# A two-layer Perceiver block on one core: turned context rows kept in memory for cross attention, image rows in parts of 512, 512 and 500

## The chip, the cores and the metric

The kernel runs on one core of one Trainium2 chip. The metric is device time in microseconds (us) of one execution. TensorE multiplies matrices, VectorE (DVE) does reductions and elementwise work, ScalarE (ACT) evaluates functions and copies, GpSimd (POOL) issues the indirect gathers, and SyncE (SP) issues most loads. SP and ACT each feed one DMA queue (q1 and q10 in the profile), POOL feeds q0; all of them run on the same 16 DMA engines.

## What is computed

There are 16 batches of 64 latent rows of width 256 and one context of 1601 rows of width 256 per batch: 77 text rows first, then 1524 image rows. All values are float32.

```python
x = x + deformable_cross_attention(layernorm(x), ctx)   # layer 0: K, V of all 1601 context rows, 5 sampled rows per head and query
x = x + sigmoid_self_attention(layernorm(x))
x = x + moe_gelu(layernorm(x))                          # 8 experts, 2 chosen
x = x + cross_attention(layernorm(x), ctx)              # layer 1, 16 heads of 64:
#   softmax over the 77 text rows + softmax over the 1524 image rows, each with its own K and V weights
x = x + state_space_block(layernorm(x))
x = x + moe_swiglu(layernorm(x))                        # 32 experts, 4 chosen, and a shared one
```

The change touches two places that read the same context: the projection of all context rows to keys and values in layer 0, and the image half of the cross attention in layer 1.

## The kernel before

The latents are 8 tiles of 128 rows (two batches each) that stay in on-chip memory (`x4`). The order of the instructions on TensorE, DVE and ACT is written out by hand; SP and POOL are ordered by a planner, which takes instructions in the order of the program as their buffers become free in its own reckoning, so SP can run ahead of the compute engines until a load's buffer isn't free. Each engine then runs its list strictly in order, the issuing of DMAs included.

**Key/value stage** (`keys_values`, lines 386 to 428). The context is cut into `spans` (line 237): per batch three spans of 512 rows and one of the 65 rows left over. A span of 512 is loaded to the tile `cx` with 4 neighbouring rows in each of 128 partitions (`cx_load`, three buffers, on SP). A span is worked on in steps of two row groups: TensorE transposes blocks of 128 x 128 (`transposes`, line 153), ACT copies them to `cxt` (line 415, three buffers), and one span later `project` multiplies them by the joint weights of all heads (`st<-wkv,cxt`, line 88, into one of four PSUM banks `st`) and ACT copies keys and values to `kv` (line 399, four buffers). When a span is complete, ACT issues its write to a table in memory (`tab`, line 402, one table for two batches), 512 bytes for each head and group of four rows. There are 7 such steps in a batch. Beside them run, in the same hand-written order: the sampling positions, the gathers of table rows (POOL, line 446, released by DVE's copy `ig`, line 444), the attention on gathered rows (`attend`), the text keys and values for layer 1 (`texts`), and, later, the dense part of layer 0 for the first tiles (`attention`, `middle`, whose weights are the tiles `w`). `tick` paces gathers and attention: it counts planned microseconds, starts a gather every 16 of them and places the attention 42 after its second gather.

**Change of stage** (lines 1590 to 1613). The pool `kvp` is given back, pools `xq` and `xc` take its memory, `cr.loads(0)` loads the image rows of batch 0, the remaining `mids` run, and `cr.begin` prepares the first pair of heads.

**Cross attention** (`class Cross`, lines 924 to 1202). A step `n` handles batch `n // 8` and a pair of heads, 128 steps in all. The image rows lie on chip twice. `cn` (two buffers, loaded by `loads` one batch ahead) has them as rows, 11 neighbouring rows per partition plus a last group of 116 partitions with one row, and a column of ones. `cT` (one buffer) has them transposed, made from `cn` by `turn`: 24 transposes on TensorE into PSUM, evicted by DVE and ACT. A step computes 12 blocks of scores from `cT` and the folded queries `qf` (three `st` banks of 4 blocks), takes maxima on DVE (line 1107), turns them (line 1126) and broadcasts them (line 1136), subtracts (line 1147), exponentiates on ACT (line 1148), and multiplies the exponentials `pt` of the step before with `cn` (`product`, line 1076). In the last step of a batch (`hp == 7`), after `out`, `turn` makes the next batch's `cT` (line 1119); `begin` makes the first one. Some steps carry parts of the next tiles' layers (`side`, `mid`, `more`, `late`).

Of the kernel before, what the change touches and what calls it, by code (L numbers as in the profile page):

```python
# [11 lines left out]
AF = mybir.ActivationFunctionType  # L12
ALU = mybir.AluOpType
# [4 lines left out]
P = 128  # L18
B, S, D = 16, 64, 256
M = 1601  # L20
# [14 lines left out]
H1, HD1, INNER, TEXT = 16, 64, 1024, 77  # L35
IMG = M - TEXT
NHP = H1 // 2
CM = IMG // P
CR = IMG - CM * P
NCH = CM + 1  # L40
NB = NCH // 4


NST, NCONV = 16, 4
# [21 lines left out]
def perceiver_kernel(ctx: ExitStack, tc: tile.TileContext, a: dict, out: bass.AP):  # L66
    nc = tc.nc

    def mk(pool, shape, tag, dtype=F32, bufs=None):
        return pool.tile(list(shape), dtype, tag=tag, name=tag, bufs=bufs)  # L70
# [9 lines left out]
    def copy(i, o, x):  # L80
        if i % 2:
            nc.scalar.copy(o, x)  # L82
        else:
            nc.vector.tensor_copy(o, x)

    def mm(o, pairs):
        for i, (l, r) in enumerate(pairs):
            nc.tensor.matmul(o, lhsT=l, rhs=r, start=i == 0, stop=i == len(pairs) - 1)  # L88
# [59 lines left out]
    def transposes(blocks, ncol=P):  # L148

        rows = blocks[0].shape[0]  # L150
        t = bank().rearrange("p (i n) -> p i n", n=P)
        for i, b in enumerate(blocks):
            nc.tensor.transpose(t[:ncol, i, :rows], b, ident[:rows, :rows])  # L153
        return t
# [79 lines left out]
    sp = tpp  # L234


    spans = [(b, m0, RP if M - m0 >= RP * P else 1) for b in range(B) for m0 in range(0, M, RP * P)]
    cxs = {}

    def cx_load(i):  # L240
        if i < len(spans):
            b, m0, r = spans[i]
            w = min(P, M - m0)
# [142 lines left out]
    def keys_values():  # L386

        held = kv = None

        def project(i, cxt, q):  # L390
            nonlocal kv
            b, m0, r = spans[i]
            w = min(P, M - m0)
            if q == 0:
                kv = mk(kvp, [P, H0, RP, 2 * HD0], "kv", bufs=4)
            for c in range(2 * q, min(2 * q + 2, r)):
                pk = big()
                mm(pk[:w], [(cxt[:, c, k, :w], wkv[:, k, :]) for k in range(KC)])
                nc.scalar.copy(kv[:w, :, c, :], pk[:w].rearrange("p (h e) -> p h e", h=H0))  # L399
            if 2 * q + 2 >= r:  # L400
                tab = tables[b // 2].rearrange("n e -> (n e)").rearrange("(b h m e) -> b h m e", b=2, h=H0, e=2 * HD0)
                nc.scalar.dma_start(
                    out=tab[b % 2, :, m0 : m0 + w * r, :].rearrange("h (p r) e -> p h (r e)", r=r),
                    in_=kv[:w, :, :r, :].rearrange("p h r e -> p h (r e)"),
                )

        for i, (b, m0, r) in enumerate(spans):
            w = min(P, M - m0)
            cx = cxs.pop(i)
            cxt = mk(kvp, [P, RP, KC, P], "cxt", bufs=3)  # L410
            steps = (r + 1) // 2
            for q in range(steps):
                m = min(2, r - 2 * q)
                tp = transposes([cx[:w, 2 * q + t, k * P : (k + 1) * P] for t in range(m) for k in range(KC)])
                nc.scalar.copy(  # L415
                    cxt[:, 2 * q : 2 * q + m, :, :w].rearrange("p r k n -> p (r k) n"), tp[:, : KC * m, :w]
                )
                if q + 1 == steps:
                    cx_load(i + 3)
                if held:  # L420
                    for part in range((held[2] + 1) // 2):
                        if min(part, steps - 1) == q:
                            project(held[0], held[1], part)
                yield
            held = (i, cxt, r)
        for q in range((held[2] + 1) // 2):
            project(held[0], held[1], q)
        yield
# [495 lines left out]
    class Cross:  # L924
# [7 lines left out]
        def loads(self, b):  # L932
            if b >= B:
                return

            cn = self.cn[b] = mk(self.xc, [P, NCH, D + 1], "cn", bufs=2)
            nc.gpsimd.memset(cn[:, :, D:], 1.0)  # L937
            nc.sync.dma_start(
                out=cn[:, :CM, :D], in_=a["ctx"][b, TEXT : TEXT + CM * P, :].rearrange("(p c) d -> p c d", c=CM)
            )  # L940
            nc.sync.dma_start(out=cn[:CR, CM, :D], in_=a["ctx"][b, TEXT + CM * P :, :])

        def text_loads(self, b):
            if b >= B:
# [9 lines left out]
        def turn(self, b):  # L954

            if b >= B:
                return
            cn = self.cn[b]
            ct = self.ctx[b] = mk(self.xc, [P, KC, NCH * P], "cT", bufs=1)
            i = 0  # L960
            for k in range(KC):
                d = slice(k * P, (k + 1) * P)
                for c in range(0, CM, 4):
                    n = min(4, CM - c)
                    blocks = [cn[:, c + i_, d] for i_ in range(n)]
                    tp = transposes(blocks)
                    copy(i % 3, ct[:, k, c * P : (c + n) * P].rearrange("p (i n) -> p i n", n=P), tp[:, :n, :])
                    i += 1
                tp = transposes([cn[:CR, CM, d]])
                nc.scalar.copy(ct[:, k, CM * P : IMG], tp[:, 0, :CR])  # L970

                nc.scalar.copy(ct[:, k, IMG:], ct[:, k, : NCH * P - IMG])

        def queries(self, t, part):

# [94 lines left out]
        def product(self, n, part, po):  # L1070

            b = n // NHP
            pt, cn = pts[n % 2], self.cn[b]
            for c in range(part * 4, part * 4 + 4):
                w = P if c < CM else CR
                nc.tensor.matmul(po, lhsT=pt[:w, c, :], rhs=cn[:w, c, :], start=c == 0, stop=c == NCH - 1)  # L1076

        def turn_out(self, n):
# [8 lines left out]
        def step(self, side=None, mid=None, more=None, late=None):  # L1087
# [11 lines left out]
            for i in range(NB):  # L1099
                if live:  # L1100
                    s = big().rearrange("p (c n) -> p c n", n=P)
                    for c in range(4):
                        j = (i * 4 + c) * P
                        mm(s[:, c, :], [(ct[:, k, j : j + P], qf[:, k, :]) for k in range(KC)])
                    st.append(s)
                if live:
                    nc.vector.tensor_reduce(mp_[:, i, :], s.rearrange("p c n -> p n c"), AX.X, ALU.max)  # L1107
                    if i:
                        nc.vector.tensor_tensor(mp_[:, 0, :], mp_[:, 0, :], mp_[:, i, :], ALU.max)
                if i == 1 and n - 2 < last:  # L1110
# [30 lines left out]
            if live:  # L1141
                pt = pts[n % 2]
                for i in range(NB):
                    c0 = i * 4
                    m = 4 if i + 1 < NB else 3
                    o = pt[:, c0 : c0 + m, :]
                    nc.vector.tensor_tensor(o, st[i][:, :m, :], mc.to_broadcast([P, m, P]), ALU.subtract)  # L1147
                    nc.scalar.activation(o, o, AF.Exp)  # L1148
                o = pt[:CR, CM, :]
                nc.vector.tensor_tensor(o, st[-1][:CR, 3, :], mc[:CR, 0, :], ALU.subtract)  # L1150
                nc.scalar.activation(o, o, AF.Exp)
            if late is not None:
                next(late, None)
            if old:
# [29 lines left out]
        def begin(self, xp):  # L1184
            self.xp = xp
            self.text_loads(0)
            self.weights(0, 0)
            yield
            for part in range(3):
                self.queries(0, part)  # L1190
                yield
            self.turn(0)
            self.loads(1)
            yield
            self.text(0, 0)
# [348 lines left out]
    with tc.manual_schedule(engines={ET.PE, ET.DVE, ET.Activation}):  # L1544
# [49 lines left out]
        for i in range(2):  # L1594
            qbds.append(mk(xq, [P, NHP, 2, 2, S], f"qbd{i}"))
            nc.gpsimd.memset(qbds[i], 0.0)
            pts.append(mk(xq, [P, NCH, P], f"pt{i}"))
            nc.gpsimd.memset(pts[i][:, CM, :], 0.0)
        xc = sx.enter_context(tc.tile_pool(name="xc", bufs=1))
        cr = Cross(xc)  # L1600
        cr.loads(0)
        while mids:
            if attended() < mids[0][0]:
                tick(2.4)
            mid()
# [156 lines left out]
```

## Time and profile before

| what | us |
|---|---|
| median of 3 runs | 3048.33 (3040.24 to 3052.96) |
| profiled execution, its own time | 3041.33 |
| its span, first to last instruction | 3039.6 |
| TensorE busy | 2840.8 |
| key/value stage | 0 to 589.5 |
| rest of the first tiles' layer 0 | 589.5 to 763 |
| cross attention steps | 763 to 2743 |

The span is the time from the first to the last instruction of the one execution that the profiler recorded. "Busy" is the union of an engine's instructions; matmuls are pipelined, so the duration of one (278 ns for a score matmul) is longer than its share of the time. Every float32 matmul shows as two instructions; a transpose is one. A square bracket in a timeline row gives the engine's idle time before the instruction and what ended it. In the DMA view a queue's row gives its packets, the megabytes, and the time of its packets as a share of what 16 engines have. The packets of four bytes among them are the completion writes of a transfer.

### The profile page before, as it was taken

The numbers are of one execution on the slowest core, as the hardware profiler recorded it, in microseconds if no ns is written. First come the engines' busy times: TensorE is split into PE (matmuls) and PEld (weight loads), VectorE is DVE, ScalarE is ACT, GpSimd is POOL, SyncE is SP. The second block draws the span as 40 slices with busy tenths as digits, with TensorE's granted clock in tenths as the row PEclk, the third lists the DMA queues.
The fourth block names the chain that finished last, engine by engine and source line by source line (L and its number), as shares of the span: only waits on it lengthen the run. The fifth ranks groups of instructions, "written<-read, shape, count | busy, mean of one in ns | idle before, by whom it ended". The sixth has DMA issues, their size and how long they took to land.

```text
span 3039.6 us, 46506 instructions
## 1 busy us (share of the span) xinstructions
PE 2840.8 (93%) x17734; PEld 2354.4 (77%) x17734; DVE 1615.9 (53%) x4137; ACT 1032.8 (34%) x2375; POOL 816.6 (27%) x923
## 2 busy tenths in 40 slices
PE   8999999966999998789979999999999999998889
PEld 4554446656898987679979999899999999886666
DVE  3332133244676665533236765686544785646756
ACT  3433444333223223324323332343233442222421
POOL 0655545566677720000010110011000010002620
PEclk9999999978999999899989999999999999999999
DMA  7666856636121220135512111122111221004983
GB/s 227 175 195 215 245 166 178 200 111 185 31 69 50 71 82 18 40 105 178 186 53 75 45 55 60 28 81 68 37 33 46 61 67 50 8 1 153 293 240 112
DMA packets 337608, 326.05 MB, mean 107 GB/s; under 512 B 58966, under 2 KB 288634, under 8 KB 336874
## 3 DMA queue, kind: packets, MB, share of 16 engines
q1 hardware_dynamic: 184889, 225.11, 23.5%
q10 hardware_dynamic: 126928, 63.06, 7.2%
q0 software_dynamic: 25568, 34.91, 5.2%
q8 instruction: 141, 2.31, 0.3%
q14 instruction: 82, 0.66, 0.1%
HBM read 248.37 MB, written 74.62 MB: 106 GB/s over the span
## 4 chain that ended last, share of the span: by engine, by line
PE 80%; DVE 9%; DMA 4%; ACT 3%; issue 1%; POOL 1%; ACTq 0%; SPq 0%; DVEq 0%; POOLq 0%
PE st L88 34%; PE mm L1076 21%; PE mm L88 16%; PE mm L153 5%; PE mm L1032 2%; DMA wg<-in_guT 2%; POOL g L446 1%; PE mm L1062 1%; DVE mp L1107 1%; DVE hs L1315 1%; PE mm L1001 1%; PE mm L1126 1%; DMA yk<-y0d,sli 1%; DVE pt L1147 1%; ACT pt L1148 0%
## 5 line engine op out<-in xcount | busy, mean ns | idle before, releaser
L1076 PE MATMUL mm<-cn,pt 128*128 128x257 f32 (+1 forms) x3072 | 748.8, 388 | 0.2 <-ACT cT L82 0.2
L88 PE MATMUL st<-qf,cT 128*128 128x128 f32 x6144 | 741.2, 278 | 0.9 <-ACT qf L1035 0.9
L446 POOL DMA_INDIRECT g<-tab,ig x640 | 613.8, 959 | 467.5 <-DVE ig L444 181.5
L88 PEld LDWEIGHTS st<-qf,cT 128*128 128x128 f32 x6144 | 722.8, 195 | 5.4 <-ACT qf L1035 1.5
L1076 PEld LDWEIGHTS mm<-cn,pt 128*128 128x128 f32 (+1 forms) x3072 | 559.5, 192 | 84.5 <-issue 0.8
L88 PE MATMUL st<-wkv,cxt 128*128 128x512 f32 (+1 forms) x832 | 380.1, 602 | 3.3 <-ACT cxt L415 3.3
L1107 DVE TENSOR_REDUCE mp<-st 128x128 f32<-128x512 f32 x384 | 260.4, 687 | 213.3 <-PE st L88 212.9
L1147 DVE TENSOR_TENSOR pt<-st,mc 128x512 f32<-128x512 f32 (+1 forms) x384 | 224.0, 638 | 159.0 <-ACT mc L1138 159.0
L88 PEld LDWEIGHTS st<-wkv,cxt 128*128 128x128 f32 (+1 forms) x832 | 150.8, 190 | 162.6 <-issue 158.4
L1148 ACT ACTIVATE pt<-pt 128x512 f32<-128x512 f32 (+1 forms) x384 | 208.0, 588 | 52.1 <-DVE pt L1147 51.8
L399 ACT COPY kv<-st 128x512 f32<-128x512 f32 (+1 forms) x208 | 121.7, 587 | 202.2 <-PE st L88 201.1
L1138 ACT COPY mc<-mm 128x128 f32<-128x128 f32 x128 | 34.2, 267 | 398.8 <-PE mm L1136 398.3
L1085 ACT COPY ot<-mm 128x256 f32<-128x256 f32 x128 | 47.6, 372 | 343.3 <-PE mm L153 343.2
L937 POOL MEMSET cn<- 128x12 f32 x16 | 1.9, 122 | 527.1 <-PE mm L1076 517.3
L1128 DVE TENSOR_REDUCE xmx<-mm 128x1 f32<-128x128 f32 x128 | 37.3, 291 | 185.5 <-PE mm L1126 185.5
L1405 POOL DMA_INDIRECT xb<-xnd,row x55 | 55.7, 1013 | 263.0 <-PE mm L1062 223.3
L1321 POOL TENSOR_TENSOR mn<-mn,hc 128x512 f32<-128x512 f32 x64 | 81.6, 1274 | 160.7 <-DVE hc L1320 156.6
L1052 ACT COPY yt<-mm 128x64 f32<-128x64 f32 x128 | 27.2, 213 | 252.6 <-PE mm L88 252.6
L88 PE MATMUL mm<-xt,w 128*128 128x256 f32 (+1 forms) x512 | 94.1, 336 | 6.8 <-DMA w<-in_gate 4.6
L88 PEld LDWEIGHTS mm<-xt,w 128*128 128x128 f32 x512 | 82.5, 200 | 22.6 <-issue 10.0
L153 PEld LDWEIGHTS mm<-ident,cx 128*128 128x128 f32 (+1 forms) x416 | 52.9, 145 | 42.1 <-issue 28.4
L1315 DVE TENSOR_TENSOR_SCAN hs<-da,db 128x512 f32<-128x512 f32 x64 | 78.4, 1225 | 6.6
(455 smaller groups left out, 3885.9 us busy)
## 6 DMA issues: line engine op xcount, KB each, us to landing
tab<-kv ACTq DMA_DIRECT2D x48, 1024.0 KB
w<-in_gate SPq DMA_DIRECT2D x66, 512.0 KB
cx<-in_ctx SPq DMA_DIRECT2D x48, 512.0 KB
cn<-in_ctx SPq DMA_DIRECT2D x16, 1408.0 KB
wg<-in_guT SPq DMA_DIRECT2D x87, 256.0 KB
w<-in_lin SPq DMA_DIRECT2D x33, 512.0 KB
wk<-in_xwkiT SPq DMA_DIRECT2D x32, 512.0 KB
wd<-in_down1T SPq DMA_DIRECT2D x87, 128.0 KB
```

What stands on the lines that cost most here:

```text
L88: nc.tensor.matmul(o, lhsT=l, rhs=r, start=i == 0, stop=i == len(pairs) - 1)
L153: nc.tensor.transpose(t[:ncol, i, :rows], b, ident[:rows, :rows])
L399: nc.scalar.copy(kv[:w, :, c, :], pk[:w].rearrange("p (h e) -> p h e", h=H0))
L446: nc.gpsimd.indirect_dma_start(out=gf[:, (half * n + s) * 4 * HD0 : (half * n + s + 1) * 4 * HD0], out_offset=None, in_=tables[j], in_offs ...
L1032: nc.tensor.matmul(pf[:, k * P : (k + 1) * P], lhsT=w[:, hp % 4, k * P : (k + 1) * P], rhs=rhs, start=True, stop=True)
L1076: nc.tensor.matmul(po, lhsT=pt[:w, c, :], rhs=cn[:w, c, :], start=c == 0, stop=c == NCH - 1)
L1107: nc.vector.tensor_reduce(mp_[:, i, :], s.rearrange("p c n -> p n c"), AX.X, ALU.max)
L1147: nc.vector.tensor_tensor(o, st[i][:, :m, :], mc.to_broadcast([P, m, P]), ALU.subtract)
L1148: nc.scalar.activation(o, o, AF.Exp)
L1315: nc.vector.tensor_tensor_scan(hs.rearrange("p c n -> p (c n)"), da.rearrange("p c n -> p (c n)"), db.rearrange("p c n -> p (c n)"), 0.0, ...
L1321: nc.gpsimd.tensor_tensor(y, y, hc, ALU.add)
L1405: nc.gpsimd.indirect_dma_start(out=x, out_offset=None, in_=xnd, in_offset=bass.IndirectOffsetOnAxis(ap=tb.row[:, i : i + 1], axis=0))
```

## The change

The text rows become a span of their own, first in each batch (77 rows, one per partition), and the image rows become three spans: 512, 512 and 500 rows, the last with 125 partitions of four rows (`SPAN = (P, P, 125)`). The counts of spans, steps, transposes and projections in a batch stay as they are. After the last step of an image span, ACT also issues a write of the whole `cxt` (512 KB, 128 partitions) to a new tensor `ctd` in memory; in the span of 125 partitions it first fills the three columns left over with copies of the first three.

In cross attention the transposes of `turn` go. `turn` now issues three loads of 512 KB on SP, one for each part, into tiles `ct0` to `ct2` with one buffer each. Batch 0's are issued right after `cr.loads(0)`, no longer in `begin`. `cn` is laid out as the spans are, by three loads with 128, 128 and 125 partitions instead of two with 128 and 116; there are 12 blocks as before. The softmax works on three whole groups of four blocks, where it had two groups of four, one of three and one single block, and the memset of `pt` goes.

```diff
-CM = IMG // P
-CR = IMG - CM * P
-NCH = CM + 1
-NB = NCH // 4
+SPAN = (P, P, 125)
+NB = len(SPAN)
+NCH = NB * RP
...
-    spans = [(b, m0, RP if M - m0 >= RP * P else 1) for b in range(B) for m0 in range(0, M, RP * P)]
+    spans = [(b, m0, w, r) for b in range(B) for m0, w, r in [(0, TEXT, 1)] + [(TEXT + s * RP * P, w, RP) for s, w in enumerate(SPAN)]]
+
+    ctd = mk(dram, [B, NB, P, RP * KC * P], "ctd")
...
                 nc.scalar.copy(
                     cxt[:, 2 * q : 2 * q + m, :, :w].rearrange("p r k n -> p (r k) n"), tp[:, : KC * m, :w]
                 )
+                if r > 1 and w < P:
+
+                    nc.scalar.copy(
+                        cxt[:, 2 * q : 2 * q + m, :, w:].rearrange("p r k n -> p (r k) n"), tp[:, : KC * m, : P - w]
+                    )
                 if q + 1 == steps:
                     cx_load(i + 3)
+                    if r > 1:
+                        nc.scalar.dma_start(out=ctd[b, (m0 - TEXT) // (RP * P)], in_=cxt.rearrange("p r k n -> p (r k n)"))
...
-            nc.sync.dma_start(
-                out=cn[:, :CM, :D], in_=a["ctx"][b, TEXT : TEXT + CM * P, :].rearrange("(p c) d -> p c d", c=CM)
-            )
-            nc.sync.dma_start(out=cn[:CR, CM, :D], in_=a["ctx"][b, TEXT + CM * P :, :])
+            m0 = TEXT
+            for i, w in enumerate(SPAN):
+                nc.sync.dma_start(
+                    out=cn[:w, i * RP : (i + 1) * RP, :D], in_=a["ctx"][b, m0 : m0 + w * RP, :].rearrange("(p r) d -> p r d", r=RP)
+                )
+                m0 += w * RP
...
-            cn = self.cn[b]
-            ct = self.ctx[b] = mk(self.xc, [P, KC, NCH * P], "cT", bufs=1)
-            i = 0
-            for k in range(KC):
-                d = slice(k * P, (k + 1) * P)
-                for c in range(0, CM, 4):
-                    n = min(4, CM - c)
-                    blocks = [cn[:, c + i_, d] for i_ in range(n)]
-                    tp = transposes(blocks)
-                    copy(i % 3, ct[:, k, c * P : (c + n) * P].rearrange("p (i n) -> p i n", n=P), tp[:, :n, :])
-                    i += 1
-                tp = transposes([cn[:CR, CM, d]])
-                nc.scalar.copy(ct[:, k, CM * P : IMG], tp[:, 0, :CR])
-
-                nc.scalar.copy(ct[:, k, IMG:], ct[:, k, : NCH * P - IMG])
+            self.ctx[b] = [
+                load(self.xc, f"ct{i}", ctd[b, i].rearrange("p (r k n) -> p r k n", r=RP, k=KC), [P, RP, KC, P], 1) for i in range(NB)
+            ]
...
-                w = P if c < CM else CR
+                w = SPAN[c // RP]
...
-                        j = (i * 4 + c) * P
-                        mm(s[:, c, :], [(ct[:, k, j : j + P], qf[:, k, :]) for k in range(KC)])
+                        mm(s[:, c, :], [(ct[i][:, c, k, :], qf[:, k, :]) for k in range(KC)])
...
                 for i in range(NB):
-                    c0 = i * 4
-                    m = 4 if i + 1 < NB else 3
-                    o = pt[:, c0 : c0 + m, :]
-                    nc.vector.tensor_tensor(o, st[i][:, :m, :], mc.to_broadcast([P, m, P]), ALU.subtract)
+                    o = pt[:, i * 4 : i * 4 + 4, :]
+                    nc.vector.tensor_tensor(o, st[i], mc.to_broadcast([P, 4, P]), ALU.subtract)
                     nc.scalar.activation(o, o, AF.Exp)
-                o = pt[:CR, CM, :]
-                nc.vector.tensor_tensor(o, st[-1][:CR, 3, :], mc[:CR, 0, :], ALU.subtract)
-                nc.scalar.activation(o, o, AF.Exp)
...
-            self.turn(0)
             self.loads(1)
...
-            nc.gpsimd.memset(pts[i][:, CM, :], 0.0)
         xc = sx.enter_context(tc.tile_pool(name="xc", bufs=1))
         cr = Cross(xc)
         cr.loads(0)
+        cr.turn(0)
```

More of the change, by code (lines that the diff above doesn't have):

```diff
@@ L241, in cx_load @@
         if i < len(spans):
-            b, m0, r = spans[i]
-            w = min(P, M - m0)
+            b, m0, w, r = spans[i]
             cx = cxs[i] = mk(kvp, [P, RP, D], "cx", bufs=3)
@@ L391, in project @@
             nonlocal kv
-            b, m0, r = spans[i]
-            w = min(P, M - m0)
+            b, m0, w, r = spans[i]
             if q == 0:
@@ L405, in project @@
                 )
-        for i, (b, m0, r) in enumerate(spans):
-            w = min(P, M - m0)
+        for i, (b, m0, w, r) in enumerate(spans):
             cx = cxs.pop(i)
```

## The prediction

> **What bounds the kernel now.** The page first: TensorE is busy 93% of the span and holds 80% of the chain that ended last, so time leaves only through TensorE, and a delay counts only where TensorE ends up waiting for it.
>
> ```profile
> PE 2840.8 (93%) x17734; PEld 2354.4 (77%) x17734; DVE 1615.9 (53%) x4137; ACT 1032.8 (34%) x2375; POOL 816.6 (27%) x923
> PE 80%; DVE 9%; DMA 4%; ACT 3%; issue 1%; POOL 1%; ACTq 0%; SPq 0%; DVEq 0%; POOLq 0%
> ```
>
> Then the timeline of TensorE at a batch's end in cross attention. The transposes of `turn` stand bare between two groups of matmuls:
>
> ```profile
> 2619.27 0.45 PE L88 MATMUL mm<-ot,wvi 128*64 128x64 f32 x6
> 2619.65 2.96 PE L153 MATMUL mm<-ident,cn 128*128 128x128 f32 x24
> 2622.53 2.01 PE L1076 MATMUL mm<-cn,pt 128*128 128x257 f32 x8
> ```
>
> They take 2.88 us from start to next start. Read likewise, the fifteen boundaries inside the stage take 2.88 to 3.75 us, 47.5 us in sum.
>
> Third, the key/value stage (0 to 589.5 us) cut at the end of each batch, since the change loads it. Columns: stretch and its length; busy time of PE, PEld, DVE, ACT, POOL; granted clock; mean share of the 16 DMA engines; GB/s.
>
> ```profile
> 42.40:75.50 33.10, 33.10 (x125) 19.36 (x124) 15.14 (x52) 11.31 (x21) 0.00 (x0) 1.00 0.67 193
> 179.10:223.10 44.00, 44.00 (x158) 26.57 (x157) 14.56 (x48) 17.25 (x36) 17.71 (x19) 1.00 0.57 175
> 308.50:338.10 29.60, 26.27 (x77) 12.39 (x76) 6.49 (x21) 11.02 (x21) 13.22 (x14) 0.94 0.90 271
> 338.10:363.20 25.10, 25.10 (x81) 12.21 (x80) 6.29 (x19) 11.20 (x21) 12.60 (x13) 1.00 0.77 214
> 388.40:429.10 40.70, 36.36 (x116) 19.31 (x115) 17.01 (x54) 15.40 (x29) 19.18 (x20) 0.92 0.51 144
> ```
>
> TensorE is full, but the DMA engines are used 51 to 90%: this is where the change can turn the bound. Where they reach 0.90, TensorE already loses 3.3 us, by way of an issue that holds ScalarE's queue for 5.92 us:
>
> ```profile
> 305.86 0.37 ACTq L402 DMA_DIRECT2D tab<-kv  x1
> ...
> 308.54 5.92 ACTq L402 DMA_DIRECT2D tab<-kv  x1
> 314.49 1.07 ACT L415 COPY cxt<-mm 128x512 f32<-128x512 f32 x2 [6.82 <-issue]
> ```
>
> **Removed: `turn`.** Fifteen boundaries give back 47.5 us. The row maxima (two DVE steps, 0.69 and 0.29 us) must then be ready within `out` and the first product (0.65 + 1.74 us); where DVE is behind, steps without a turn show gaps of 0.24 us, so I leave 1 us: **-46.5**. The sixteenth turn, in `begin`, has 1.69 us on the chain: **-1.7**. Its evictions (64 DVE copies, 39.7 us; 96 on ACT, 33.7 us) lie under TensorE: 0. Likewise the softmax in three whole groups: DVE 128 x (684 - 547 - 279) ns = -18 us, ACT -22 us, both hidden by the product of the pair before: 0.
>
> **Added in cross attention.** Per batch three 512 KB reloads on SP's queue. Each part has one buffer, free once the last pair's scores have read it: about 2, 4 and 6 us into a step of 15.6 - 2.9 = 12.8 us, and needed 12.8, 14.7 and 16.6 us after that start. An isolated 512 KB load (`wk`, issued 1013.05) has its last packet 3.5 us after issue. Waiting behind the reloads on SP: the next `wk`, `cn`, `vt`, needed a step or more later. Margin over 6 us: 0, with 5 us per late boundary if SP stands in another wait.
>
> **Added in the key/value stage.** ACT issues 48 writes of 512 KB (0.37 us each) and makes 32 small copies (0.21 us, as L972): 24 us over 590 us in which ACT is busy 42%; hidden by the four `st` buffers, some 6 us of matmuls. The transfers are another matter. DMA views of two short stretches, one holding a 128-row table write (48 such) and a 128-row `cx` load, one a 65-row table write:
>
> ```profile
> q10 hardware_dynamic: 2064, 1.05, 44.7%
> q1 hardware_dynamic: 144, 0.52, 21.7%
> ```
>
> ```profile
> q10 hardware_dynamic: 1053, 0.13, 10.0%
> ```
>
> 2064 is 128 x 16 packets of 512 B and 16 more; 144 is 128 and 16; but 1053 is 65 x 16 = 1040 and **13** more. The extra ones are completion writes, one from each engine that took part: 65 rows were spread over 13 engines, not 16. A third stretch with 128-, 77- and 116-row loads agrees (1632 = 1408 + 16 + 77 + 11 + 116 + 4). The Trainium skill says this as a rule (DMA: Bandwidth & Descriptors, section "Why a DMA increments its semaphore by 16 and not by 1"): a copy uses the largest number of engines up to 16 that divides the size of its slowest dimension. No 125-row transfer is in the trace. Going by the nearest row in size (128 rows, 16 engines), the new spans cost what the old ones do; going by the rule, which three counts support, **125 = 5 x 5 x 5 gets five engines**. I take the rule; the row would lead to rival (a), 3015 us.
>
> From those rows (8 us stretch): a 1 MB table write is 0.447 x 8 = 3.58 us of all 16 engines, a 512 KB load in 4 KB packets 0.217 x 8 = 1.74 us. On five engines the 125-row table write takes 3.58 x 16/5 x 125/128 = 11.2 us, the `cx` load 5.4 us. What a batch adds to each of these five:
> - table write of the third part: 11.2 - 3.6 = 7.6 us
> - its `cx` load: 5.4 - 1.7 = 3.7 us
> - three turned writes (128 partitions, all engines; priced as loads): 3 x 1.74 = 5.2 us
> - text of 77 rows on 11 engines for 65 on 13: 0.5 us
>
> Together 17 us, on top of share x length: 22.2 + 17 = 39.2 us in a 33.1 us stretch, 19.3 + 17 = 36.3 in 25.1, 26.6 + 17 = 43.6 in 29.6, 25.1 + 17 = 42.1 in 44.0. Over the sixteen stretches what exceeds the length adds to 82 us, less 7 because the first batch's third write falls into the second: 75 us if the five engines never idle. They must idle some: **+80** (bounds 40, if packets run faster with eleven engines quiet, and 125). Buffers can't absorb it: three `cxt`, four `kv`, and ACT's queue itself, where an issue waits for room and cxt copies, `kv` copies and the activations of the feed-forward wait behind it, and TensorE for them.
>
> **Moved: text first.** The same seven steps a batch, in another order, with the same transposes, matmuls and copies: 0. POOL's first gather (79.0 us) waits for the last table write of batch 1, now one of 11 us; the attention that uses it is placed 42 us of planned time behind it, so 0, and at most the delay of some 9 us if that cover were gone. `turn(0)` moves up to the end of this stage and onto SP's queue, its source long written. And the last write of the stage is now the slow one. At the change of stage SP waits for it, the loads following in order:
>
> ```profile
> 592.73 0.65 SPq L938 DMA_DIRECT2D cn<-in_ctx  x1
> 593.44 1.15 SPq L941 DMA_DIRECT2D cn<-in_ctx  x1
> 594.69 4.08 SPq L158 DMA_DIRECT2D w<-in_gate  x2
> ...
> 604.04 2.18 PE L88 MATMUL mm<-xt,w 128*128 128x256 f32 x9 [2.22 <-DMA w<-in_gate]
> ```
>
> `cn` waits for the table writes (memory reused), released at 592.65, 3.2 us after the last issue; with 11.2 us of transfer that is some 9 us later. Three turned loads (5.2 us) go ahead of `w`, and `cn`'s 125-row part costs 3 us on five engines. TensorE waits for `w`: 0 to 18 us, **+14**.
>
> **Sum.** -46.5 - 1.7 + 80 + 14 = +45.8. The profiled execution took 3041.3 us (span 3039.6), giving 3087; it stands 7 us under the median of three, so the forecast for a median is 3048.3 + 45.8 = **3094 us**, its own range 3065 to 3130.
>
> **Rivals.** (a) The 125-row transfers spread as 128-row ones, or the surplus hides. Then the stage adds 4.8 us per engine and batch, which fits below 1.0 nearly everywhere (some 9 us lost around 300 to 390), and 6 us at the change of stage: -48.2 + 15, 3015 us. For it: TensorE's full row; against: 13, 11 and 4 engines. It decides once stage and transition together lose less than 48.2 us. (b) ScalarE is held. A third table write puts 400 packets on each of five engines; the fullest that any issue here went ahead at is about 205 per engine (at 305.86, its own 2048 packets and some 1230 of the write before). At 28 ns a packet the other 195 hold ACT 5.5 us, 8 with the other queues' share; TensorE has about 3 us of work ahead. 15 x 3 to 5 us on top where the engines aren't the limit already: 3140. (c) Half the surplus is absorbed: 3048 + 5, within noise. (d) Reloads late by 5 us at every boundary: +75, 3169; against it the margin above.
>
> **Chances.** Forecast 0.50, (b) 0.20, (c) 0.14, (a) 0.11, (d) 0.05. 0.5% is about what a measurement can tell. Faster 0.11, same 0.14, slower 0.75. The range leaves out most of (a), below, and the far ends of (b) and (d), above: 3040 to 3150.
>
> **What would show it.** Third-part table writes with 2000 + 5 packets; the key/value stage ending near 670 instead of 590, its DMA share falling in the mean; ACT issues of several us; no `ident,cn` transposes and last steps of 12.8 us. If the stage ends by 605, the spread over five engines, or its price, was wrong.

## The result, and the profile after

The changed kernel takes **3092.49 us** (median of 4 runs, 3090.28 to 3099.89); the kernel before, run beside it, 3050.39 us. The ratio is **1.015, with a 95% interval of 1.0129 to 1.017**: slower by 1.3 to 1.7%. The forecast was 3094 us, +45.8; measured +42.1. Of the chips that the experiments ran on, two were slower: every kernel took some 8% longer there, the kernel before too (3295 and 3299 us), so each run is read by its ratio to the kernel before on the same chip. Lengths of stages and waits come from one recorded execution of each kernel.

First the page of the changed kernel: the busy times of the engines, and the chain that ended last.

```profile
PE 2812.0 (91%) x17350; PEld 2321.4 (75%) x17350; DVE 1572.9 (51%) x3945; ACT 999.2 (32%) x2183; POOL 814.3 (26%) x921
PE 77%; DVE 9%; DMA 5%; ACTq 3%; ACT 3%; issue 1%; POOL 1%; SPq 0%; DVEq 0%; POOLq 0%
```

TensorE has 384 instructions and 29 us of work less than before, as it should with 16 turns of 24 transposes gone. But its share fell from 93 to 91%, and ScalarE's queue (ACTq), which was 0% of the chain, now holds 3% of it: 3% of 3088.6 us is some 90 us in which the end waited for ScalarE to hand on a transfer.

The span grew by 49.0 us. The places where it changed, from the ends of the same TensorE instructions in both traces (us; last projection, first scores, last product of an image block):

| stage | before | after | difference |
|---|---|---|---|
| key/value stage | 588.8 | 671.9 | +83.1 |
| change of stage, to the first scores | 174.1 | 186.3 | +12.2 |
| cross attention | 1979.6 | 1929.9 | -49.7 |
| what follows | 297.1 | 300.5 | +3.4 |

**Cross attention.** The timeline of TensorE in the same step as the one shown of before (the last of a batch, number 119, now begun at 2663.45):

```profile
2669.50 0.45 PE L87 MATMUL mm<-ot,wvi 128*64 128x64 f32 x6
2669.88 2.01 PE L1071 MATMUL mm<-cn,pt 128*128 128x257 f32 x8
```

The `ident,cn` row is gone, and the product follows at once. The step took 16.36 us and takes 13.47.

**The key/value stage.** The two stages whole, before and then after. Columns: window and its length; busy time of PE, PEld, DVE, ACT, POOL, each with its count; granted TensorE clock; mean share of the 16 DMA engines; GB/s.

```profile
0.00:588.80 588.80, 565.13 (x1901) 312.35 (x1902) 179.83 (x589) 245.27 (x463) 279.63 (x306) 0.99 0.66 197
```

```profile
0.00:671.90 671.90, 581.33 (x1901) 319.59 (x1902) 179.04 (x589) 243.54 (x495) 282.85 (x310) 0.94 0.69 210
```

The same 1901 TensorE instructions fill 565 of 589 us before and 581 of 672 after. TensorE's idle time went from 23.7 to 90.6 us, +67; the other 16 us are the same matmuls running longer, at a mean granted clock of 0.94 instead of 0.99. So 67 us of pauses went with a loss of 83 us. What TensorE waited for, from the waits of after (total, times, longest; three lines of the list):

```profile
PE st L87 <- ACT cxt L413: 36.5, 5, 17.1
PE mm L152 <- DMA cx<-in_ctx: 10.1, 2, 6.3
PE mm L87 <- ACT kts L544: 9.4, 2, 5.2
```

Before, the first of these was 3.3 us, once; the wait for `cx` was 9.1 us and is nearly unchanged. It is copies on ScalarE that are late. The timeline of ScalarE and TensorE at the third batch shows why:

```profile
118.46 0.28 ACTq L401 DMA_DIRECT2D tab<-kv  x1
...
121.05 6.69 ACTq L401 DMA_DIRECT2D tab<-kv  x1
121.11 0.38 PE L152 MATMUL mm<-ident,vtw 128*128 128x128 f32 x2
127.78 0.65 ACT L534 COPY tt<-mm 128x256 f32<-128x256 f32 x2 [6.76 <-issue]
128.20 0.69 PE L152 MATMUL mm<-ident,vtw 128*128 128x128 f32 x2 [6.71 <-ACT tt L534]
```

At 118.46 ScalarE issues the 125-row table write, and that takes it 0.28 us. At 121.05 it issues the next transfer, the small write of the 77 text rows, and stands in this one issue for 6.69 us. The copy `tt` behind it waits for nothing but the issue, and TensorE waits 6.71 us for `tt`. This comes in each of the fifteen batches that have text rows of the next batch behind them: 3.9 to 10.1 us, once 20.1, and 114 us in all beyond 0.4 us each. Other issues, mostly the turned write that follows, add 28 us.

TensorE's pauses stand at these holds. Of its 90.6 us of idle time, 72 lie inside an issue of ScalarE's of more than 1 us or in the 1.5 us after it, and all of them at the 14 issues of 4.9 us and more. The 17 shorter ones, of up to 3.9 us, have next to none (0.1 us). Before, the same count gives 4.8 of 23.7 us.

**The 125-row write.** The DMA view of 16 us at the end of the stage, where nothing else is on ScalarE's queue (packets, MB, share of 16 engines):

```profile
q10 hardware_dynamic: 2005, 1.02, 23.4%
```

2000 data packets and 5 completion writes: five engines. Their first packet starts at 673.39, their last at 687.69, and 23.4% of 16 engines for 16 us is 59.9 us, 12.0 us for each of five.

**The change of stage**, SP's queue, one issue of ScalarE's and TensorE:

```profile
672.55 0.28 ACTq L401 DMA_DIRECT2D tab<-kv  x1
...
688.35 2.27 SPq L945 DMA_DIRECT2D cn<-in_ctx  x3
690.66 3.06 SPq L157 DMA_DIRECT2D ct<-ctd  x3
693.84 0.40 SPq L157 DMA_DIRECT2D w<-in_gate  x1
...
706.80 9.06 PE L87 MATMUL mm<-xt,w 128*128 128x256 f32 x32 [14.06 <-DMA w<-in_gate]
```

`cn` goes out 15.8 us after the last table write's issue, where it was 3.2; the three turned loads stand ahead of `w`; and TensorE waits 14.06 us for `w` instead of 2.22.

### The profile page after: what moved, and what is told of

Same layout as the page of the kernel before. It is cut to its first block, busy times and chain, and to the rows that moved or that the text cites. A ratio compares the mean times of both kernels' runs of the same rounds, so it can differ in the third digit from the quotient of the medians.

```text
span 3088.6 us, 45612 instructions
## 1 busy us (share of the span) xinstructions
PE 2812.0 (91%) x17350; PEld 2321.4 (75%) x17350; DVE 1572.9 (51%) x3945; ACT 999.2 (32%) x2183; POOL 814.3 (26%) x921
## 4 chain that ended last, share of the span: by engine, by line
PE 77%; DVE 9%; DMA 5%; ACTq 3%; ACT 3%; issue 1%; POOL 1%; SPq 0%; DVEq 0%; POOLq 0%
PE st L87 34%; PE mm L1071 21%; PE mm L87 15%; ACTq L401 3%; PE mm L152 3%; PE mm L1027 2%; DMA wg<-in_guT 2%; POOL g L451 1%; PE mm L1057 1%; DVE hs L1303 1%; DVE mp L1101 1%; DMA tab<-kv 1%; PE mm L996 1%; PE mm L1120 1%; DMA w<-in_gate 1%
## 5 line engine op out<-in xcount | busy, mean ns | idle before, releaser
L87 PE MATMUL st<-qf,ct 128*128 128x128 f32 x6144 | 740.4, 278 | 0.9 <-ACT qf L1030 0.9
L87 PEld LDWEIGHTS st<-qf,ct 128*128 128x128 f32 x6144 | 722.2, 194 | 5.4 <-ACT qf L1030 1.5
L87 PE MATMUL st<-wkv,cxt 128*128 128x512 f32 (+2 forms) x832 | 389.1, 614 | 36.5 <-ACT cxt L413 36.5
L1139 DVE TENSOR_TENSOR pt<-st,mc 128x512 f32<-128x512 f32 x384 | 241.1, 683 | 157.3 <-ACT mc L1132 157.3
L87 PEld LDWEIGHTS st<-wkv,cxt 128*128 128x128 f32 (+2 forms) x832 | 153.9, 194 | 201.8 <-issue 162.9
L1140 ACT ACTIVATE pt<-pt 128x512 f32<-128x512 f32 x384 | 229.6, 628 | 50.7 <-DVE pt L1139 50.4
L398 ACT COPY kv<-st 128x512 f32<-128x512 f32 (+2 forms) x208 | 120.1, 588 | 170.8 <-PE st L87 158.9
L87 PE MATMUL mm<-xt,w 128*128 128x256 f32 (+1 forms) x512 | 96.1, 341 | 18.4 <-DMA w<-in_gate 15.8
L87 PEld LDWEIGHTS mm<-xt,w 128*128 128x128 f32 x512 | 83.9, 203 | 34.6 <-issue 23.7
L413 ACT COPY cxt<-mm 128x512 f32<-128x512 f32 (+2 forms) x112 | 61.1, 545 | 114.8 <-issue 68.0
```

The costliest lines, as they stand in the source:

```text
L413: nc.scalar.copy(cxt[:, 2 * q : 2 * q + m, :, :w].rearrange("p r k n -> p (r k) n"), tp[:, : KC * m, :w])
L1139: nc.vector.tensor_tensor(o, st[i], mc.to_broadcast([P, 4, P]), ALU.subtract)
```

## The experiments

The total came out as forecast, but these lines don't look like the forecast's reason. It said that five engines have more work than a batch lasts (theory A in the expectations). The trace shows an in-order ScalarE held at an issue (theory C), which the forecast had as a rival, on top of the load and not in its place. The two share the 125-row write, so the total can't tell them apart. The runs do. (Theory B in the expectations puts the cost on the turned writes.)

### The 125-row transfers cut

All three kinds of 125-row transfer (context load `cx`, table write, `cn`) as 112 rows and 13 rows. Bytes, order and queues stay.

```diff
+def cuts(w):
+    return [(0, w)] if w % 16 == 0 or w < 100 else [(0, w - w % 16), (w - w % 16, w)]
...
-                nc.scalar.dma_start(
-                    out=tab[b % 2, :, m0 : m0 + w * r, :].rearrange("h (p r) e -> p h (r e)", r=r),
-                    in_=kv[:w, :, :r, :].rearrange("p h r e -> p h (r e)"),
-                )
+                for p0, p1 in cuts(w):
+                    nc.scalar.dma_start(
+                        out=tab[b % 2, :, m0 + p0 * r : m0 + p1 * r, :].rearrange("h (p r) e -> p h (r e)", r=r),
+                        in_=kv[p0:p1, :, :r, :].rearrange("p h r e -> p h (r e)"),
+                    )
```

> Every 125-row transfer (cx load, table write, cn load) is cut into 112 + 13 rows, which divide over 16 and 13 engines; all else as in the changed kernel. Theory A (125 rows run on five DMA engines, and those five set the pace of the key/value stage): the last table write is issued near 600 us instead of 672, no issue of ScalarE's holds it over 3 us outside the stretch around 310, and the time is 3005 to 3025. Theory B (the 25 MB of turned writes on ScalarE's queue are the cost, on however many engines): the stage still ends at 655 or later, the time is 3070 or more.

Measured: 3013.41 us against 3049.68, ratio 0.9876 (0.9854 to 0.9899). The whole key/value stage, and ScalarE's issues at the third batch:

```profile
0.00:598.90 598.90, 565.17 (x1901) 311.86 (x1902) 179.29 (x589) 245.71 (x495) 284.47 (x310) 0.99 0.79 235
```

```profile
107.55 2.07 ACTq L408 DMA_DIRECT2D tab<-kv  x2
...
111.30 0.30 ACTq L408 DMA_DIRECT2D tab<-kv  x1
```

The stage is 598.9 us long, 73 us shorter than after, with TensorE's busy time and clock back at the values of before. The 16 DMA engines are used more (0.79), not less. The completion writes on ScalarE's queue up to 20 us after the stage number 1952, after 1568: 384 more, as 16 batches of 16 + 13 instead of 5 give. The pair of issues takes 2.07 us and the text write 0.30, where it was 6.69; three other issues still take 3.1 to 4.0 us. So the shape of the 125-row transfers costs the change 73 us. What is left, +10 us over before, is what the rest costs together: the turned writes, the small copies, the additional issues and the new order. Theory B is out: the turned writes are all there, and the stage doesn't end at 655 or later. At the change of stage TensorE waits 3.51 us for `w`.

Only the table write cut; `cx` and `cn` stay on five engines. The diff is the second half of the one above.

> Only the table write of the 125-row part is cut into 112 + 13 rows; its cx and cn loads stay on five engines. Theory A: each of the five carries 7.6 us less a batch, 9.4 us more than before the change instead of 17, which exceeds the length of the stretches by about 25 us in sum: stage end 605 to 620, time 3015 to 3040. If it is the loads that matter most (they hold up the transposes), it stays above 3060. Theory B: no gain.

Measured: 3028.43 us, ratio 0.9938 (0.9921 to 0.9956). The stage:

```profile
0.00:613.80 613.80, 570.45 (x1901) 314.84 (x1902) 179.62 (x589) 245.08 (x495) 283.49 (x310) 0.97 0.76 230
```

58 of the 73 us come from the table write alone. The `cx` loads on five engines cost the other 15 in this stage.

### The same load, another queue

The whole 125-row table write, still on five engines, issued by SP instead of ScalarE:

```diff
-                nc.scalar.dma_start(
+                (nc.sync if r > 1 and w < P else nc.scalar).dma_start(
```

> The 125-row table write is issued by SP instead of ScalarE, otherwise the changed kernel. Theory A with the five engines' load as the limit: the load is the same, SP is held instead and the cx loads behind it come late; stage end 640 to 680, time 3060 to 3100. Theory C (the load would fit, but ScalarE is held at the issue and its copies come late): stage end near 610, time 3020 to 3040.

Measured: 3032.86 us, ratio 0.9947 (0.9929 to 0.9964). The stage; then one batch on SP's queue and on ScalarE's; then TensorE's longest wait:

```profile
0.00:618.70 618.70, 573.34 (x1901) 315.50 (x1902) 179.36 (x589) 245.09 (x495) 284.48 (x310) 0.97 0.74 228
```

```profile
457.00 0.28 SPq L401 DMA_DIRECT2D tab<-kv  x1
460.73 9.40 SPq L245 DMA_DIRECT2D cx<-in_ctx  x2
```

```profile
460.02 0.31 ACTq L401 DMA_DIRECT2D tab<-kv  x1
463.39 0.33 ACTq L424 DMA_DIRECT2D ctd<-cxt  x1
```

```profile
PE mm L152 <- DMA cx<-in_ctx: 26.4, 6, 7.4
```

Not a byte is moved otherwise, and five engines do what they did, yet the stage is 53 us shorter than after (618.7 against 671.9). This decides it: **53 of the 83 us go with ScalarE being held**, not with the load. The hold itself has not gone. It moved with the write to SP: in this batch the next transfer there, the load of `cx`, stands for 8.24 us. In the whole stage SP's issues take 169 us beyond 0.4 us each, where they took 11 after, and ScalarE's 24 instead of 142. That harms less, because SP runs ahead, with three `cx` buffers, and has no arithmetic to do. It isn't free either: TensorE's wait for `cx` grows from 10.1 to 26.4 us.

The other way round, less load with ScalarE as before: the new spans, but `turn` kept on TensorE, with no turned writes and no turned loads.

```diff
-                    if r > 1:
-                        nc.scalar.dma_start(out=ctd[b, (m0 - TEXT) // (RP * P)], in_=cxt.rearrange("p r k n -> p (r k n)"))
...
+            for i, w in enumerate(SPAN):
+                for q in range(2):
+                    tp = transposes([cn[:w, i * RP + 2 * q + t, k * P : (k + 1) * P] for t in range(2) for k in range(KC)])
+                    o = cts[i][:, 2 * q : 2 * q + 2].rearrange("p r k n -> p (r k) n")
+                    copy(j % 3, o[:, :, :w], tp[:, :, :w])
```

> The spans of the changed kernel (77, 512, 512, 500 rows) with no turned writes and no reloads: cross attention turns its rows from cn on TensorE as before. Theory A: the five engines still carry 11.8 us more a batch, the stage ends 40 to 60 us later than before, and nothing is gained in cross attention: 3090 to 3115, that is as slow as the changed kernel or slower. Theory B: the stage ends near 590 and the time is that of before, 3040 to 3060.

Measured: 3124.82 us, ratio 1.0251 (1.0227 to 1.0276), the slowest of all: it has the loss of the first stage, and its cross attention (1967.2 us) is only 12 us shorter than before, where the changed kernel's is 50. The stage, and the same issue as above:

```profile
0.00:672.30 672.30, 588.13 (x1901) 323.04 (x1902) 178.59 (x589) 241.58 (x463) 284.18 (x310) 0.94 0.59 172
```

```profile
119.67 6.80 ACTq L400 DMA_DIRECT2D tab<-kv  x1
126.52 0.65 ACT L526 COPY tt<-mm 128x256 f32<-128x256 f32 x2 [6.88 <-issue]
```

The DMA share fell from 0.69 to 0.59, some 67 us of work for each of the 16 engines, and the stage is as long as after (672.3 and 671.9). If the load set its length, it would have shrunk. The hold is 6.80 us, where it was 6.69. Neither theory had the size right: A expected 40 to 60 us more than before, B none, and it is 83.5.

A similar trial moved the text rows' write to SP, so that the issue which is held in the changed kernel isn't ScalarE's any more:

```diff
-                nc.scalar.dma_start(
+                (nc.sync if r == 1 else nc.scalar).dma_start(
```

> The changed kernel with one difference: the table write of the 77 text rows, which is the issue that ScalarE is held at (about 7 us in each batch, behind the 125-row write in the same queue), is issued by SP. The 125-row write stays on ScalarE's queue and on five engines, so the load of the five is that of the changed kernel. Theory A (the load of the five is the limit): stage end above 650 us, ratio to before above 1.008. Theory C (a held ScalarE is the loss): no issue of ScalarE's over 4 us outside the stretch around 350, stage end 610 to 625, ratio 0.990 to 0.998.

Measured on one of the slower chips: 3268.42 us against 3299.41, ratio 0.9919 (0.9894 to 0.9943). SP's queue and ScalarE in one batch:

```profile
244.93 0.32 SPq L401 DMA_DIRECT2D tab<-kv  x1
```

```profile
240.71 0.35 ACTq L401 DMA_DIRECT2D tab<-kv  x1
...
247.45 7.98 ACTq L424 DMA_DIRECT2D ctd<-cxt  x1
255.47 0.73 ACT L544 COPY kts<-mm 128x308 f32<-128x308 f32 x2 [8.05 <-PE st L87]
```

The text write goes out on SP in 0.32 us, four microseconds behind the same big write, whose packets are then still on the five engines. What is held is the next transfer on ScalarE's own queue, wherever it comes: the turned write, 6.7 us after the big one, for 7.98 us. So the hold belongs to the queue that has the big write; the other queue isn't held. With that, the expectation that no issue of ScalarE's would exceed 4 us failed: they still add to 86 us beyond 0.4 us each. The ratio is in theory C's range, but the stage (718.5 us) can't be compared, as neither the kernel before nor the changed kernel was recorded on that chip. The size of the gain is left open.

### Smaller pieces

For batches 2 to 14, the 125-row write as five writes of 25 rows (also five engines), two at once and the others one by one at the next steps. Load and queue stay; what is waiting at a time gets less.

```diff
+                late = r > 1 and w < P and 1 < b < B - 1
...
+                if late:
+                    write(0, 25)
+                    write(25, 50)
+                    rest.extend([lambda p0=p0: write(p0, p0 + 25) for p0 in (50, 75, 100)])
+                else:
+                    write(0, w)
...
+                if rest:
+                    rest.pop(0)()
```

> The changed kernel, but in batches 2 to 14 the table write of the 125-row part goes out as five writes of 25 rows, two at once and three in the three steps after. 25 rows too divide over five engines, so the load on the five engines is that of the changed kernel and only the holding of ScalarE goes. Theory A (the load on the five is the limit): stage end above 650 us, time above 3070. Theory C (ScalarE held at the issue is the loss): issues of about 0.4 us, stage end 605 to 625, time 3015 to 3045.

Measured on a slower chip: 3297.74 us, ratio 1.000 (0.9978 to 1.0023). It was run again on a chip that isn't slow:

> The same kernel as e7_pieces, on another chip: on the chip of the first look all engines paused for up to 10 us with nothing shown that they waited for, in the kernel before too (3295 us there), and such pauses cover a held ScalarE. Theory A (the load on the five engines is the limit): stage end above 650 us, ratio to before above 1.008. Theory C (ScalarE held at the issue is the loss): stage end 605 to 625, ratio 0.99 to 1.0.

Measured: 3053.70 us against 3045.89, ratio 1.0022 (1.0012 to 1.0032). The stage, and ScalarE's timeline in a batch:

```profile
0.00:631.50 631.50, 573.44 (x1901) 315.07 (x1902) 179.20 (x589) 243.80 (x495) 284.65 (x310) 0.97 0.73 223
```

```profile
368.63 5.13 ACTq L405 DMA_DIRECT2D tab<-kv  x2
373.80 0.59 ACT L424 COPY cxt<-mm 128x512 f32<-128x512 f32 x1 [5.20 <-issue]
373.82 2.19 ACTq L405 DMA_DIRECT2D tab<-kv  x1
...
376.74 1.42 ACTq L405 DMA_DIRECT2D tab<-kv  x1
378.20 0.59 ACT L424 COPY cxt<-mm 128x512 f32<-128x512 f32 x1 [1.49 <-issue]
```

40 us of the stage come back, with the load on the five engines as it was. That lies between the two theories: A expected a stage of over 650 us, C of 605 to 625 with issues of about 0.4 us. The holds haven't gone, they are cut up, and copies come between them. ScalarE's issues beyond 0.4 us each still add to 106 us, against 142 after, and TensorE's idle time falls from 90.6 to 58.1 us. The two fall by about as much, so this run doesn't tell whether shorter holds help or only less of them. Here short holds cost time too, as they follow each other closely: 24 us of TensorE's pauses stand at the 50 issues of 1 to 4 us, counted as above. With the pieces the change is worth about nothing.

### The order at the change of stage, and what the turned rows are worth

The cut transfers of the first experiment, with `turn(0)` back in `begin`, behind the loads of `w`:

```diff
+            self.turn(0)
             self.loads(1)
...
-        cr.turn(0)
```

> Every 125-row transfer cut into 112 + 13 rows, and the first reload of turned rows (batch 0) issued in begin, as the first turn was before, not at the change of stage. If the three loads ahead of the feed-forward weights cost there, the time between the last key/value matmul and the first score falls from 179.0 us (all cut, reload early) toward 174.1 us (before), and the whole to 3005 to 3012. If they don't, it stays at 3010 to 3018.

Measured: 3269.63 us against 3295.21, ratio 0.9921 (0.9891 to 0.9952). A second time, on a further chip:

> All 125-row transfers cut into 112 + 13 rows and the first reload in begin, on another chip than in the first look at it. If the early reload costs at the change of stage: first score 174 to 176 us after the last key/value matmul (179.0 with the early reload) and a ratio to before of 0.984 to 0.988. If not, the ratio stays at 0.987 to 0.990.

Measured: 3256.92 us against 3299.41, ratio 0.9879 (0.9839 to 0.9919). Against 0.9876 for the first experiment on the faster chip this shows no gain. TensorE's largest pause at the change of stage doesn't end on `w` in either trace, but the wait for `w` was 3.51 us already with the cut transfers. Both runs are on the slower chips, where the change of stage took 203.2 and 223.2 us (179.0 in the first experiment), so a few microseconds can't be told there; it stays open.

The cut transfers with `turn` kept on TensorE and no turned writes, as in the run with less load:

> The spans of 77, 512, 512 and 500 rows with every 125-row transfer cut into 112 + 13 rows, no turned writes and no reloads: cross attention turns its rows from cn on TensorE. If text first and the new span sizes cost nothing by themselves, the stage ends near 589 and the time is 3040 to 3058. If the order itself costs, 3065 or more.

Measured: 3295.55 us, ratio 1.0002 (0.9976 to 1.0028), beside 0.9921 for the kernel with turned rows, on the same chip. Again, beside its repeat:

> The new spans, all 125-row transfers cut into 112 + 13 rows, no turned writes or reloads, on another chip than in the first look. If text first and the new sizes cost nothing by themselves: stage end 586 to 594, ratio 0.997 to 1.003.

Measured: 3272.99 us, ratio 0.992 (0.9891 to 0.995), beside 0.9879. Cross attention is 30 and 28 us longer than in the kernel with turned rows on the same chip. On the faster chip the run with less load shows the same: 1967.2 us against 1929.9, 37 us. The sum of the stages isn't clear: the key/value stage is 5 us shorter without turned rows in one pair and 28 in the other, and the two pairs of ratios put the turned rows' worth at 0.8% and at 0.4%, the second with intervals that overlap. Whether the new order and spans cost anything by themselves isn't settled either: the first ratio says no, the second was expected at 0.997 to 1.003 and is below. The waits of TensorE in the second show what disturbs the reading:

```profile
PE mm L1129 <- DVE mp L1112: 48.8, 19, 16.4
PE st L92 <- issue: 34.8, 44, 4.3
```

The first wait is longer than on the faster chips (31.2 us before, with one pause of 17.2 there too). The second is new: in this trace 68 us of TensorE's pauses end on "issue", nothing that the trace shows, and in the traces of before, of after and of the first experiment none do. Comparisons of less than 1% were not to be had there.

Last, the turned writes of the kernel with turned rows and the late `turn(0)`, issued by SP instead of ScalarE:

```diff
-                        nc.scalar.dma_start(out=ctd[b, (m0 - TEXT) // (RP * P)], in_=cxt.rearrange("p r k n -> p (r k n)"))
+                        nc.sync.dma_start(out=ctd[b, (m0 - TEXT) // (RP * P)], in_=cxt.rearrange("p r k n -> p (r k n)"))
```

> As the kernel with all transfers cut and the late first reload, but the turned rows are written from SP's queue instead of ScalarE's. If the remaining 10 us of the stage come from ScalarE being held behind the turned writes, the stage ends 5 to 10 us earlier: 3000 to 3008. If SP, waiting for ScalarE's copies, holds up the cx loads behind it, it ends later: 3015 or more.

Measured: 3268.72 us, ratio 0.9919 (0.9888 to 0.9949), the same as 0.9921 with ScalarE issuing them. Once the 125-row transfers are cut, it makes no difference that can be measured there which queue hands on the turned rows.

## Why the prediction was right, and where it was not

**The total** was right: +45.8 forecast, +42.1 measured, with the forecast's own sum +83.1 + 12.2 - 49.7 + 3.4 = +49.0 in the profiled execution. That the sum fits is in part luck: its largest term stood for the wrong cause, as is told below. The last term was not forecast; the other kernels on that kind of chip end with 297 to 302 us after cross attention, in no order of their edits.

**Removed turns.** Forecast -46.5 over the fifteen boundaries. The fifteen last steps are 46.0 us shorter, the very last 1.7 and the other steps 2.0. The work that was said to hide the maxima hides them: among the last steps TensorE has a gap of 0.52 us in the steps 7, 15 and 23, and of 3.5 us, as before, in step 31. The turned reloads never end a wait of TensorE, so rival (d) fell. Not all of the gain is the turned rows: with the same spans and `turn` on TensorE, cross attention is 37 us longer than in the changed kernel, and 12 us shorter than before. What gives those 12 us was not taken apart.

**Five engines.** The count was right, 2000 + 5 packets, where the nearest row in size would have given 16 completions. So the rule of the Trainium skill (DMA: Bandwidth & Descriptors, section "Why a DMA increments its semaphore by 16 and not by 1") held for this case against the row of 128 partitions. The price held too: 11.2 us forecast, 12.0 measured. Rival (a) fell on this count and comes true when the transfers are cut: it gave 3015 us, and the first experiment took 3013. (Its 4.8 us for each engine and batch should be about 5.2 by the forecast's own rows, three turned writes of 1.74.) Rival (c) fell too: the two stages together lost 95 us.

**+80 for the load of five engines: right in size (83), wrong in its reason.** This is the step that failed: "what exceeds the length adds to 82 us, less 7 ...: 75 us if the five engines never idle". The load isn't what exceeds the stretches. With the load unchanged and only the issuing queue another, the stage lost 30 us and not 80; with 67 us less of it for each engine the stage lost the same 83. The parts, each the difference of two stage lengths: 10 us for turned writes and the rest (first experiment), 15 for `cx` on five engines (second), about 5 for the table write's load (the third, with late `cx` loads included), and 53 for ScalarE held (after less the third). Taken away in another order, the parts might divide somewhat otherwise. Two things made the sum too large. A turned write was priced as a load, 1.74 us; its 128 packets take 163.6 ns each, 1.31 us. More important, the sum of packet times isn't a limit for an engine here: with the write on SP, the share of 0.74 over 618.7 us and 11.4 us more a batch for five engines (7.7 for the write, 3.7 for `cx`) make 458 + 182 = 640 us by the prediction's own accounting, in a stage of 618.7. That is an estimate, since the trace doesn't name the engine of a packet. The DMA view of after from 120.0 to 127.5, in the middle of a 125-row write, says the same:

```profile
q10 hardware_dynamic: 1382, 0.71, 33.0%
q0 software_dynamic: 172, 0.18, 11.9%
```

ScalarE's queue moved nothing else then. 33.0% of 16 engines is 5.28 engines' time, and it was on five; POOL's gathers ran beside it. So the times of an engine's packets overlap, and an engine takes more in a stretch than their sum allows.

**Rival (b), ScalarE held**, had the right mechanism and a wrong place in the sum. It forecast a hold of 5.5 to 8 us, and 3.9 to 10 were measured. It was charged 3 to 5 us a batch, on top, "where the engines aren't the limit already". They are not, so it is the main term: 53 / 15 = 3.5 us a batch (45 of the 53 as idle time of TensorE, 8 as longer matmuls). Where it put the hold was wrong: not the big write's own issue stands (0.28 us) but the next one on its queue. The line that showed this was in the prediction: at 305.86 a 128-row write goes out in 0.37 us, and the 65-row write behind it, at 308.54, takes the 5.92. It was read as "an issue that holds ScalarE's queue", without asking which. The count behind the rival was wrong too, as the last section shows: the packets of the new transfer don't add to those of the old.

**Change of stage.** Forecast +14 less 1.7, so +12.3; measured +12.2. SP's wait is 10.7 us, released 12.6 us later than before relative to the last issue (9 forecast), and TensorE's wait rose by 11.8 us.

**The signs named.** The stage's end near 670 (671.9), ScalarE's issues of several us, no transposes and the shorter steps all came. "Its DMA share falling in the mean" did not: it rose from 0.66 to 0.69. The 48 turned writes add 63 us to each engine (without them the share was 0.59), and the forecast left them out of that sentence.

## What to carry to other kernels

Give a transfer a row count with 16 as a divisor (here 128 and 112 rows ran on 16 engines, 125 on five; the completion writes tell), or cut it so that its large part has one: 112 + 13 rows in place of 125, with not a byte changed, turned a change that loses 1.5% into one that gains 1.2%, and it is faster than both kernels. When a slow transfer is put on the queue of an engine that also computes, look at the next transfer behind it there and at the copies behind that one, and price the hold of the issuing engine, not only the load of the DMA engines: here 53 us and some 20. Two theories that give the same total need a run which changes one and not the other: here, the same transfer on another queue.

## What was not expected of the hardware

A transfer on few engines doesn't hold its own issue, it holds the next one on the same queue, however small. When the hold shown above ended, at 127.74, 546 of the big write's 2000 packets had not started, 109 on each of five engines. In the fifteen holds of this kind 419 to 565 are left, 84 to 113 an engine. What the next transfer brings hardly matters. The text write brings 112 packets to each of its 11 engines (77 rows x 16 packets), the turned write 8 to each of 16. In the run with the text on SP, the turned write that took 7.98 us waited until 485 were left. With the big write on SP, the `cx` load at 460.73 waited until 579 were. The 65-row write before the change, held for 5.92 us, waited until 1279 packets of a 128-row write were left, 80 on each of 16 engines. So what counts is how much of the earlier write is left. Rival (b) instead added both and let 205 pass. Why the limit lies there, no run here shows. The other queue was not held at such a time: four microseconds behind the big write SP handed on a table write in 0.32 us.

Pauses of TensorE went with a loss of more than their length: in this stage 67 us more of idle time went with 16 us more of busy time for the same instructions, at a mean granted clock of 0.94 instead of 0.99. In the trace the clock is either 1.00 or 0.5. Before, it stood at 0.5 for 13.7 us of the stage, in three stretches of 3.4 or 6.8 us; after, for 78.5 us in eleven, of 3.4 to 17.1 us. Each of the eleven begins in a pause of 2.6 us or more, or within half a microsecond of its end.
